# Where the gamma folds, two sums of x and the Strassen weight sums sit among the first fifteen slots of a fused cross-attention kernel

## The chip, the cores and the metric

The kernel runs on one core of one Trainium2 chip. The metric is the device time of one execution in microseconds (us). The engines are named as in the profile: PE is TensorE (PEld its weight loads), DVE is VectorE, ACT is ScalarE, POOL is GpSimd, SP is the engine that issues most of the DMAs (SPq is its queue). Each engine executes its instructions in the order in which the kernel writes them; engines wait for one another through semaphores.

## The reference

All data is fp32. `x` is 8 x 256 x 1024, `ctx` is 8 x 256 x 1024 and serves as keys and values of 32 heads of 32 columns.

```python
mu, var = mean(x), variance(x)                       # over the last axis
xn   = (x - mu) * rsqrt(var + 1e-5) * ln_gamma + ln_beta
Q    = split_heads(xn @ Wq.T)
K    = V = split_heads(ctx)
s    = einsum('bhsd,bhtd->bhst', Q, K) * 32 ** -0.5  # masked by mask_BxS2_bf1
attn = einsum('bhst,bhtd->bhsd', softmax(s), V)
out  = x + merge_heads(attn) @ Wout.T
```

## The kernel before

**Slots.** The work is cut into N = 64 slots: 8 batches of NQ = 8 groups of four heads. The loop `for n in range(N)` (L938) writes the instructions of all engines by hand, in the order in which they run (a manual schedule). Slot n does this, in this order:

- PE: `scores(n + 1)` (L485, 16 matmuls into four PSUM banks tagged "sc", one for each head), steps of the output projection of an earlier batch (`product_steps`, L704), `values(n - 2)` (L630, the products with V), then query projections for later slots (`make_q`, L336, or `query_product`, L444).
- `softmax(n + 1)` (L506). For each head j the DVE adds the mask and takes the minimum (`exps`, L530), ACT takes the exponent and its sum (L534), DVE takes the reciprocal (L541), POOL multiplies by it (L548, `normalize`; in slots up to 13 head 3 is done by ACT, L544), DVE transposes 32 x 32 blocks into `pT` (`blocks`, L554), ACT copies half of them aside (`aside`, L560), and SP moves blocks between partitions in four DMAs (L616, L620). The last part, `tail`, is written behind the first `exps` of the next softmax as long as n is under 8, and at once from n = 8 on. A list `fill` holds other work, dealt out one item at a time between these steps.
- Behind the softmax come, in this order: sums of attention outputs (`sum_at`, L698, POOL), layer norm of later x (`ln_stats`, L217, DVE with a small power on POOL, L235; `ln_norm` on ACT, L248), moves of x blocks by SP (`move_x`, L321), saves of weight sums to DRAM (`keep_wq`, L405, SP), sums of x (`sum_x`, L436, POOL), the fold (`fold`, L364, POOL) and the weight sums listed in `sums[n]` (L850 to L864).

A head's PSUM bank of scores is free for the next slot's scores once its two L530 instructions have read it; there are four banks, and each slot fills all four.

**Gamma.** Batch 0 multiplies by gamma where x is transposed (`copy_x0`). From batch 1 on the scaled gamma is folded into `wq`, in place, when batch 0 has used a block of it. `fold(o)` does row block o in one POOL instruction of 128 x 1024; it is called at the end of slots 0 to 3 for o = n. Row blocks 4 to 7 are done by `fold_late`, eight DVE instructions of 128 x 512 (L373), as items of `fill` in slots 4 and 5.

**Strassen.** The output projection and, from batch 2 on, the query projection are 2 x 2 block products with seven multiplications (Strassen-Winograd). The sums of weight blocks T1 to T4 are made once: `sum_wo` (L182, for Wout) and `sum_wq` (L403, for Wq), each an elementwise 128 x 512 instruction, on the engine that the lists name. The sums of x (S1, S2, S4, S3 of `sum_x`, L442, 128 x 512 each) are made for every batch from 2 on. Batch 2's query products run in slots 10 (S1), 11 (S4), 12, 13 (S2), 14 (S3), 15 and 16; batch 0's output projection runs in slots 9 to 16.

**Slots 8 to 10 around the change.** In slot 8 the two x sums S1 and S2 of batch 2 stand at the end, behind the DMAs of `move_x` that slot 7 issues. Slot 9 ends with two wo sums on DVE (L182) and two wq sums on POOL (L403). In slot 10 `add_p1` (L755, POOL) adds a kept product to the residual tile `r`, `store` (L764, DVE) adds the PSUM bank "po" to the same tile, and only then may the next four projection steps (`po_S`, L722) overwrite that bank.

Of the kernel before, what the change touches and what calls it, by code (L numbers as in the profile page):

```python
# [49 lines left out]
ALU = mybir.AluOpType  # L50
# [9 lines left out]
def xattn_kernel(  # L60
# [10 lines left out]
    nc = tc.nc  # L71
# [4 lines left out]
    NQ = NC  # L76
# [8 lines left out]
    NEG_SCALE = -1.0 / math.sqrt(HD)  # L85
# [21 lines left out]
    NK = D // P // 2  # L107
# [134 lines left out]
    def ln_norm(b, s, engine):  # L242
        if engine is nc.scalar:
            shift = sm.tile([P, 1], F32, tag="shift", name=f"shift_{b}_{s}", bufs=2)
            nc.gpsimd.tensor_scalar(
                shift, mvs[b][:, s, 0:1], rstds[b][:, s : s + 1], -1.0, ALU.mult, ALU.mult
            )
            engine.activation(  # L248
                xs[b][:, s, :], xs[b][:, s, :], AF.Identity,
                bias=shift, scale=rstds[b][:, s : s + 1],  # L250
            )
            return
        engine.tensor_scalar(
            xs[b][:, s, :], xs[b][:, s, :], mvs[b][:, s, 0:1], rstds[b][:, s : s + 1],
            ALU.subtract, ALU.mult,
        )
# [107 lines left out]
    def fold(o):  # L364

        nc.gpsimd.tensor_tensor(
            wq[:, o], wq[:, o], gs.unsqueeze(2).to_broadcast([P, NC, P]), ALU.mult
        )

    def fold_late(*chunks):  # L370

        for c in chunks:
            nc.vector.tensor_scalar(  # L373
                wq[:, ds(NK, NK), c], wq[:, ds(NK, NK), c], gs[:, c : c + 1], None, ALU.mult
            )

# [471 lines left out]
    sums = {n: [] for n in range(N)}  # L850
    for n, engine, which, *chunks in (
        (1, nc.gpsimd, T3, 0), (2, nc.gpsimd, T3, 1), (4, nc.gpsimd, T2, 0, 1),
        (4, nc.gpsimd, T3, 2), (5, nc.gpsimd, T3, 3), (5, nc.gpsimd, T2, 2, 3),
        (6, nc.gpsimd, T4, 0), (7, nc.gpsimd, T4, 1), (9, nc.vector, T4, 2, 3),
        (10, nc.vector, T1, 0, 1), (13, nc.gpsimd, T1, 2), (14, nc.gpsimd, T1, 3),
    ):
        sums[n] += [partial(sum_wo, which, c, engine) for c in chunks]
    for n, engine, which, *chunks in (
        (6, nc.gpsimd, "T1", 0, 1), (7, nc.gpsimd, "T1", 2, 3), (9, nc.gpsimd, "T2", 0, 1),
        (10, nc.gpsimd, "T2", 2), (11, nc.gpsimd, "T2", 3), (11, nc.gpsimd, "T3", 0),  # L860
        (12, nc.gpsimd, "T3", 1, 2), (13, nc.gpsimd, "T3", 3), (13, nc.vector, "T4", 0),
        (14, nc.vector, "T4", 1, 2), (14, nc.gpsimd, "T4", 3),
    ):
        sums[n] += [partial(sum_wq, which, o, engine) for o in chunks]  # L864

# [3 lines left out]

    away, rings = {n: [] for n in range(N)}, {n: [] for n in range(N)}  # L870
    for n, name, half in (
        (7, "T1", 0), (8, "T1", 1), (9, "B11", 0), (10, "B11", 1), (13, "T3", 0), (14, "T3", 1),
    ):
        away[n].append(partial(keep_wq, name, half))
    for n, b in firsts.items():
# [37 lines left out]
    for _ in first:  # L913
        pass
    ln_norm(1, 1, nc.vector)


    steps, evacuations = {}, {n: [] for n in range(N + 1)}
# [19 lines left out]
    for n in range(N):  # L938
        b, i = divmod(n - NQ, NQ)
        new_q = new_qs[n]  # L940
        between = []
        if n % 2 and n + 1 < N:
            between.append(partial(load_v, n + 1))
        elif n % 2 == 0 and n + 4 < N:
            between.append(partial(load_k, n + 4))
        ahead = rings[n]
        if n + 3 in firsts or n + 2 in firsts:
            between, ahead = between + ahead, []
        if b >= 0:
            if b == B - 2 and i - 1 in (5, 6):  # L950
                between.append(partial(send, b, *ENDS_TO[i - 1]))
            if i < 4:
                between.append(partial(load_res, b, *((0, 0), (0, 1), (1, 1), (1, 0))[i]))
        between += [partial(load_x, *args) for args in loads[n]]
        between += [partial(load_mask, one) for one in masks[n]]
        if n in (3, 4):
            between.append(partial(load_wo, B21, n - 3))
        if n == N - 4:
            again = xp.tile([P, NS, D], F32, tag="x", name="x_again")
            for s in range(NS):  # L960
                between.append(partial(nc.sync.dma_start, again[:, s, :], x[B - 1, ts(s, P), :]))

        if n + 1 < N:
            scores(n + 1)
        project_steps(n, 0)
        hooks, now, behind = {}, [], []
        for what, one, *args in evacuations[n]:
            if one == B - 2:
                now.append(partial(what, one, *args))
            else:  # L970
                place = 0 if i in (3, 4, 6) or i < 3 and what is not add_p1 else "soon" if i == 2 else 1
                hooks.setdefault(place, []).append(partial(what, one, *args))
        if n >= 2:
            values(n - 2)
        project_steps(n, 1)
        copies = [partial(copy_q, q) for q in new_q]
        if n in halves and n % 2 == 0:
            make_q(halves[n], second=True, chunks=range(NC // 2, NC))
            copies.insert(0, partial(copy_q, halves[n]))
        behind_p1 = new_q if i == 1 and b in P1_ASIDE else ()  # L980
        if behind_p1:
            copies = []
        else:
            for q in new_q:
                make_q(q)
        if n in products:
            query_product(*products[n])
            copies.append(partial(copy_product, *products[n]))
        for one in now:
            one()  # L990
        fill = []
        if n < 2:
            transpose_x1(2 * n)
            transpose_x1(2 * n + 1)
            fill = [partial(copy_x1, 2 * n), partial(copy_x1, 2 * n + 1)]
            if n == 1:
                hooks["soon"], fill = fill, []
        elif n <= NQ:
            fill = [partial(ln_stats, *args, parts=(i,)) for args in stats[n] for i in range(3)]
            fill += [partial(blocks_x, *args) for args in trans[n]]  # L1000
            fill += [partial(fold_late, *chunks) for chunks in {4: ((0, 1), (2, 3), (4, 5)), 5: ((6, 7),)}.get(n, ())]
        if n + 1 < N:
            softmax(n + 1, copies, ahead, between, hooks, fill)
            for q in behind_p1:
                make_q(q)
                copy_q(q)
        else:
            copy_at(n - 2)
            tails.pop()()
            for load in between:  # L1010
                load()
        if b >= 0 and i == 1:
            sum_at(b, "S2", *((slice(NK - 1, NK),) if b == B - 2 else ()))
        later = []
        if n > NQ:
            for args in stats[n]:
                ln_stats(*args, later=later)
        for args in norms[n]:
            ln_norm(*args, nc.scalar)
        if n > NQ:  # L1020
            for args in trans[n]:
                blocks_x(*args)
        for args in moves[n]:
            move_x(*args)
        for one in away[n]:
            one()
        for one in biases[n]:
            mask_bias(one)
        project_steps(n, 2)
        for one, slot in S3_SLOTS:  # L1030
            if n == slot:
                sum_at(one, "S3")
        if b >= 0:
            for name in {2: ("S4",), 3 if b == B - 2 else 5: ("S1",)}.get(i, ()):
                sum_at(b, name)
            if i == 0 and b == B - 2:
                sum_at(b, "S2", slice(0, NK - 1))
        for slot, name in ((n + 2, "S1"), (n + 2, "S2"), (n + 1, "S4"), (n - 1, "S3")):
            if slot in firsts:
                sum_x(firsts[slot], name)  # L1040
        if b == B - 2:
            if i > 2:
                add_kept(b, i, *ENDS_TO[i])
        elif b >= 0 and i in (3, 4, 5):
            add_p1(b, *{3: (0, 1), 4: (1, 1), 5: (1, 0)}[i])
        for one in later:
            one()
        if n in halves and n % 2:
            make_q(halves[n], second=True, chunks=range(NC // 2))
        if n == 0:  # L1050
            nc.gpsimd.tensor_scalar(gs, gam, NEG_SCALE, 1.0, ALU.mult, ALU.mult)
        if n < NK:
            fold(n)
        for one in sums[n]:
            one()
        if N - NQ + 2 < n < N - 1:

            c = n - (N - NQ + 3)
            if c == 0:
                last = ps_q.tile([P, 512], F32, tag="pq", name="po_last")  # L1060
            end_steps(last, "A11", B11, (c,), (0,))
# [101 lines left out]
```

## Time and profile before

| | us |
|---|---|
| median of 3 runs (580.30 to 580.79) | 580.46 |
| the profiled execution | 581.39 |
| its span, first to last instruction | 579.6 |
| mean granted TensorE clock, share of full | 0.991 |
| PE busy in the span | 569.3 (98%) |
| DVE busy | 473.1 (82%) |
| ACT busy | 423.7 (73%) |
| POOL busy | 389.5 (67%) |

The span is shorter than the profiled execution's own time by 1.8 us, which lie around it. The slots can be read off the PE timeline: each begins with 16 matmuls of L493. Slots 2 to 17 begin at 36.01, 43.59, 51.15, 58.69, 67.06, 80.02, 87.56, 95.10, 103.47, 117.01, 126.38, 134.88, 143.42, 151.93, 161.23 and 168.88 us, with slot 18 at 177.24. PE's busy time is modelled, so its share is read together with these beginnings. In the table by stretch the columns are the stretch, its length, then for PE, PEld, DVE, ACT and POOL the busy time with the instructions in brackets, then the granted clock, the DMA share and GB/s.

### The profile page before, as it was taken

To read this page: it belongs to the slowest core of one execution; us is meant where nothing else is said; L and a number is where in the kernel's file an instruction comes from. 1 tells how busy PE (TensorE), PEld (TensorE's weight loads), DVE (VectorE), ACT (ScalarE), POOL (GpSimd) and SP (SyncE) were. 2 spreads that over 40 slices of the span, in tenths; PEclk is the share of its full clock that TensorE was granted. 3 is DMA by queue.
4 is the path that set the end of the run, shared out by engine and by line. 5 is a ranking of instruction groups with operands and counts; after the bars stand their busy time and mean duration, and the time that the engine had idled before them with its cause. 6 is when DMAs were issued, how large, how long until landed. Compare 5 with 4: busy or idle time off the path is not lost.

```text
span 579.6 us, 20202 instructions
## 1 busy us (share of the span) xinstructions
PE 569.3 (98%) x7266; PEld 398.5 (69%) x7266; DVE 473.1 (82%) x1715; ACT 423.7 (73%) x1462; POOL 389.5 (67%) x643
## 2 busy tenths in 40 slices
PE   9999999799999999999999999999999999999997
PEld 8788686567766776667776777767776677665544
DVE  5988988798998888978889788988888768879823
ACT  3699699597677876778676886779677767769920
POOL 2477696978678665857749756686656666458780
PEclk9999889999999999999999999999999999999999
DMA  8964568744878658887668676887657855435751
GB/s 309 396 176 144 161 180 259 245 138 137 264 245 268 181 155 234 242 255 213 196 199 249 213 222 185 241 232 221 188 172 225 276 162 161 136 111 172 219 160 72
DMA packets 47219, 119.02 MB, mean 205 GB/s; under 512 B 8976, under 2 KB 9744, under 8 KB 47120
## 3 DMA queue, kind: packets, MB, share of 16 engines
q1 hardware_dynamic: 46976, 117.74, 67.9%
q8 instruction: 57, 0.93, 0.7%
q14 instruction: 42, 0.34, 0.2%
q10 hardware_dynamic: 144, 0.01, 0.0%
HBM read 66.33 MB, written 11.53 MB: 134 GB/s over the span
## 4 chain that ended last, share of the span: by engine, by line
PE 75%; DVE 7%; DMA 5%; POOL 5%; ACT 4%; issue 2%; SPq 2%; POOLq 0%; ACTq 0%; DVEq 0%
PE po_S L722 19%; PE pq_A L454 16%; PE sc L493 10%; PE pv L638 9%; PE po_A L722 8%; PE pq_S L454 6%; ACT e L534 3%; PE po_end L789 3%; DVE pT L554 2%; POOL e L548 2%; DVE e L530 2%; DMA xnT<-xe 2%; DMA pT<-pT 1%; DMA r<-in_x_dram 1%; PE po_last L789 1%
## 5 line engine op out<-in xcount | busy, mean ns | idle before, releaser
L548 POOL TENSOR_SCALAR e<-e,rden 128x256 f32<-128x256 f32 x484 | 225.1, 483 | 139.8 <-DVE rden L541 135.2
L534 ACT ACTIVATE e<-e,mn 128x256 f32<-128x256 f32 x512 | 254.0, 501 | 53.9 <-DVE mn L530 52.8
L554 DVE STREAM_TRANSPOSE pT<-e 128x512 f32<-128x512 f32 x256 | 179.3, 704 | 38.1 <-POOL e L548 33.6
L530 DVE CUSTOM_DVE_ANT_0 e<-sc,mb 128x256 f32<-128x256 f32 x512 | 185.4, 416 | 25.1 <-PE sc L493 25.1
L560 ACT COPY pc<-pT 128x512 f32<-128x512 f32 x128 | 78.9, 617 | 57.8 <-DVE pT L554 35.7
L534 ACT ACTIVATION_READ_ACCUMULATOR e<-e,mn 128x1 f32 x512 | 98.2, 192 | 0.0
L493 PEld LDWEIGHTS sc<-k,qa 32*128 32x128 f32 x1024 | 47.8, 185 | 44.9 <-issue 19.5
L493 PE MATMUL sc<-k,qa 32*128 32x256 f32 x1024 | 76.7, 404 | 1.2 <-DVE mn L530 1.1
L722 PE MATMUL po_S<-wo,at 128*128 128x512 f32 x152 | 74.4, 606 | 0.5 <-DVE r L764 0.5
L638 PE MATMUL pv<-pT,v 64*32 64x128 f32 x4096 | 74.9, 276 | 0.0
L638 PEld LDWEIGHTS pv<-pT,v 64*32 64x32 f32 x4096 | 57.6, 106 | 22.8 <-issue 11.8
L722 PE MATMUL po_A<-wo,at 128*128 128x512 f32 x128 | 59.4, 605 | 0.0
L345 PE MATMUL pq<-xnT,wq 128*128 128x256 f32 (+1 forms) x240 | 55.9, 388 | 0.2 <-POOL e L548 0.2
L722 PE MATMUL po_S<-wo,s 128*128 128x512 f32 x104 | 51.8, 623 | 4.1 <-DVE r L764 4.1
L454 PEld LDWEIGHTS pq_A<-xnT,wq 128*128 128x128 f32 x416 | 48.5, 192 | 6.2 <-issue 5.0
L345 PEld LDWEIGHTS pq<-xnT,wq 128*128 128x128 f32 x240 | 45.3, 193 | 8.9 <-issue 1.7
L454 PE MATMUL pq_A<-xnT,wq 128*128 128x128 f32 x416 | 48.5, 275 | 0.0
L541 DVE RECIPROCAL rden<-den 128x2 f32<-128x2 f32 x256 | 38.1, 150 | 11.7 <-ACT e L534 10.6
L530 DVE DVE_READ_ACCUMULATOR2_ANT mn<- 128x1 f32 x512 | 42.4, 83 | 0.0
L722 PEld LDWEIGHTS po_A<-wo,at 128*128 128x128 f32 x128 | 22.9, 189 | 25.7 <-issue 24.7
L722 PEld LDWEIGHTS po_S<-wo,at 128*128 128x128 f32 x152 | 25.5, 190 | 20.3 <-issue 19.5
L755 POOL TENSOR_TENSOR r<-r,p 128x512 f32<-128x512 f32 x24 | 30.6, 1276 | 5.6 <-DMA r<-in_x_dram 5.6
(104 smaller groups left out, 658.6 us busy)
## 6 DMA issues: line engine op xcount, KB each, us to landing
v<-in_kv_dram SPq DMA_DIRECT2D x32, 512.0 KB, 4.0
pT<-pT SPq DMA_DIRECT2D x128, 128.0 KB, 3.0
pT<-pc SPq DMA_DIRECT2D x128, 128.0 KB, 3.9
ring<-kept_T SPq DMA_DIRECT2D x20, 512.0 KB, 4.9
k<-in_kv_dram SPq DMA_DIRECT2D x32, 256.0 KB, 4.0
x<-in_x_dram SPq DMA_DIRECT2D x15, 512.0 KB, 5.9
r<-in_x_dram SPq DMA_DIRECT2D x28, 256.0 KB, 4.7
out_dram<-r SPq DMA_DIRECT2D x28, 256.0 KB, 3.6
```

What stands on the lines that cost most here:

```text
L345: nc.tensor.matmul(pqs[n], wq[:, o, c, :], xnTs[b](c), start=(c == 0), stop=(c == NC - 1),)
L454: nc.tensor.matmul(pqs[b][:, o, :], w[:, c], x_[:, c], start=begins and o + c == 0, stop=c == NK - 1, skip_group_check=True,)
L493: nc.tensor.matmul(scs[n][j][:, s, :], qa[r, n % NQ, ts(s, P)], ks[n - n % 2][r, n % 2, :], start=True, stop=True,)
L530: nc.vector.tensor_tensor_reduce(out=e[:, s, :], in0=pss[j][:, s, :], in1=mbs[n // NQ], scale=1.0, scalar=NO_SCORE, op0=ALU.add, op1=ALU.m ...
L534: nc.scalar.activation(e[:, s, :], e[:, s, :], AF.Exp, bias=mn[:, s : s + 1], scale=-1.0, accum_out=den[:, s : s + 1],)
L541: nc.vector.reciprocal(rden, dens[j])
L548: nc.gpsimd.tensor_scalar(es[j][:, s, :], es[j][:, s, :], rden[:, s : s + 1], 1.0, ALU.mult, ALU.mult,)
L554: nc.vector.transpose(pT[:, :, :, j, :, :].rearrange("p a i s k -> p (a i) s k"), es[j].rearrange("p s (b t) -> p b s t", t=K),)
L560: nc.scalar.copy(pc[:, :, ts(j, 2)], pT[:, 1, :, ts(j, 2)])
L638: nc.tensor.matmul(pvs[n][r][j * HD : (j + 1) * HD], vs[n - n % 2][ts(r, 2 * K), i, ds(n % 2 * P + j * HD, HD)], pT[ts(r, 2 * K), :, i, j, ...
L722: nc.tensor.matmul(po, operand(b, name)[:, c], wo[:, which, c], start=begins and c == 0, stop=c == NK - 1, skip_group_check=not begins,)
L755: nc.gpsimd.tensor_tensor(r, r, p1s[b], ALU.add)
```

## The change

`fold_late` goes. All eight row blocks are folded by POOL: blocks 0 and 1 (and the small scaled gamma that they need) right before the loop, behind the first softmax, and block n + 2 at the end of slots 0 to 5. For batch 2 alone, S1 and S2 of x move from the end of slot 8 to that of slot 9, and S4 from slot 9 to 10; S3 stays in slot 11. The weight sums are dealt anew: DVE does six of wo's sixteen in place of four (three in slot 9, two in slot 10, one in slot 12), POOL ten in place of twelve, and several wq sums on POOL change slots. The save of the first half of wq's T1 moves from slot 7 to slot 8.

```diff
-    def fold_late(*chunks):
-
-        for c in chunks:
-            nc.vector.tensor_scalar(
-                wq[:, ds(NK, NK), c], wq[:, ds(NK, NK), c], gs[:, c : c + 1], None, ALU.mult
-            )
...
     for n, engine, which, *chunks in (
         (1, nc.gpsimd, T3, 0), (2, nc.gpsimd, T3, 1), (4, nc.gpsimd, T2, 0, 1),
-        (4, nc.gpsimd, T3, 2), (5, nc.gpsimd, T3, 3), (5, nc.gpsimd, T2, 2, 3),
-        (6, nc.gpsimd, T4, 0), (7, nc.gpsimd, T4, 1), (9, nc.vector, T4, 2, 3),
-        (10, nc.vector, T1, 0, 1), (13, nc.gpsimd, T1, 2), (14, nc.gpsimd, T1, 3),
+        (5, nc.gpsimd, T3, 2, 3), (6, nc.gpsimd, T2, 2, 3), (9, nc.vector, T4, 0, 1, 2),
+        (10, nc.vector, T4, 3), (10, nc.vector, T1, 0), (12, nc.vector, T1, 1),
+        (13, nc.gpsimd, T1, 2), (14, nc.gpsimd, T1, 3),
     ):
         sums[n] += [partial(sum_wo, which, c, engine) for c in chunks]
     for n, engine, which, *chunks in (
-        (6, nc.gpsimd, "T1", 0, 1), (7, nc.gpsimd, "T1", 2, 3), (9, nc.gpsimd, "T2", 0, 1),
-        (10, nc.gpsimd, "T2", 2), (11, nc.gpsimd, "T2", 3), (11, nc.gpsimd, "T3", 0),
-        (12, nc.gpsimd, "T3", 1, 2), (13, nc.gpsimd, "T3", 3), (13, nc.vector, "T4", 0),
-        (14, nc.vector, "T4", 1, 2), (14, nc.gpsimd, "T4", 3),
+        (6, nc.gpsimd, "T1", 0), (7, nc.gpsimd, "T1", 1, 2, 3), (8, nc.gpsimd, "T2", 0, 1),
+        (11, nc.gpsimd, "T2", 2, 3), (12, nc.gpsimd, "T3", 0, 1, 2), (13, nc.gpsimd, "T3", 3),
+        (13, nc.vector, "T4", 0), (14, nc.vector, "T4", 1, 2), (14, nc.gpsimd, "T4", 3),
     ):
         sums[n] += [partial(sum_wq, which, o, engine) for o in chunks]
...
-        (7, "T1", 0), (8, "T1", 1), (9, "B11", 0), (10, "B11", 1), (13, "T3", 0), (14, "T3", 1),
+        (8, "T1", 0), (8, "T1", 1), (9, "B11", 0), (10, "B11", 1), (13, "T3", 0), (14, "T3", 1),
...
     ln_norm(1, 1, nc.vector)
+    nc.gpsimd.tensor_scalar(gs, gam, NEG_SCALE, 1.0, ALU.mult, ALU.mult)
+    for o in range(2):
+        fold(o)
...
-            fill += [partial(fold_late, *chunks) for chunks in {4: ((0, 1), (2, 3), (4, 5)), 5: ((6, 7),)}.get(n, ())]
...
-        for slot, name in ((n + 2, "S1"), (n + 2, "S2"), (n + 1, "S4"), (n - 1, "S3")):
-            if slot in firsts:
-                sum_x(firsts[slot], name)
+        for slot, one in firsts.items():
+            late = 1 if one == SPLIT else 0
+            for name in {-2: ("S1", "S2"), -1: ("S4",)}.get(n - slot - late, ()) + {1: ("S3",)}.get(n - slot, ()):
+                sum_x(one, name)
...
-        if n == 0:
-            nc.gpsimd.tensor_scalar(gs, gam, NEG_SCALE, 1.0, ALU.mult, ALU.mult)
-        if n < NK:
-            fold(n)
+        if n + 2 < NQ:
+            fold(n + 2)
```

Here `firsts` maps the slot of a batch's first query product to the batch (10 to batch 2), `SPLIT` is 2, `NK` is 4 and `NQ` is 8.

## The prediction

> **What bounds the kernel now.** I read the waits of PE first, then the busy times by slot, then the timeline of the two bad places and the chain that ended last. PE waits for little that the profile can name:
>
> ```profile
> PE po_S L722 <- DVE r L764: 4.7, 3, 3.3
> PE busy L119 <- POOL ring masks.py:199: 1.4, 1, 1.4
> PE sc L493 <- DVE mn L530: 1.1, 2, 0.6
> ```
>
> Busy times by slot (cut at the first score matmul of slots 5, 6, 7, 10 and 18) say more:
>
> ```profile
> core 0: us, PE busy (x) PEld busy (x) DVE busy (x) ACT busy (x) POOL busy (x), PEclk, DMA share, GB/s
> ...
> 58.69:67.06 8.37, 7.65 (x105) 6.09 (x104) 8.37 (x17) 3.98 (x13) 6.11 (x7) 1.00 0.57 174
> 67.06:80.02 12.96, 12.36 (x104) 9.02 (x105) 11.92 (x47) 11.61 (x43) 10.08 (x16) 0.74 0.64 177
> 80.02:87.56 7.54, 7.54 (x106) 6.09 (x105) 6.21 (x27) 7.43 (x26) 6.67 (x10) 1.00 0.58 152
> ...
> 103.47:117.01 13.54, 10.24 (x119) 6.80 (x118) 11.93 (x38) 8.77 (x30) 13.00 (x18) 0.87 0.65 217
> ...
> 177.24:185.75 8.51, 8.51 (x119) 6.24 (x118) 7.78 (x29) 5.96 (x22) 7.75 (x12) 1.00 0.83 250
> ```
>
> Slots 5, 6 and 7 hold the same matmuls (about 105), but only slot 7 runs at PE's own pace, 7.54 us, as slots 2 to 4 and 8 do. Slots 5 and 6 take 58.69 to 80.02 = 21.33 us where two such slots take 15.08: **6.25 us lost**, most of it at a granted clock of 0.74. Slot 10 has the matmuls of slot 18 (x119) but takes 13.54 against 8.51: **5.03 us lost**, of which 3.30 are idle and 1.48 are the next four po_S steps, slowed (3.46 against 1.98 in slot 11). Nearly everywhere else up to slot 18 PE follows PE; slot 15 idles for 0.53. So the profile offers at most 6.25 + 5.03 + 0.53 = 11.8 us, and other engines matter only where they hold up PE.
>
> Slot 5, in the timeline (start, length, engine, line):
>
> ```profile
> 61.55 4.09 POOL L182 TENSOR_TENSOR wo<-wo 128x512 f32<-128x512 f32 x3
> 61.85 2.66 DVE L373 TENSOR_SCALAR wq<-wq,gs 128x512 f32<-128x512 f32 x2
> ...
> 65.06 1.26 DVE L373 TENSOR_SCALAR wq<-wq,gs 128x512 f32<-128x512 f32 x2
> 66.25 0.41 DVE L530 CUSTOM_DVE_ANT_0 e<-sc,mb 128x256 f32<-128x256 f32 x1
> ...
> 67.06 0.69 PE L493 MATMUL sc<-k,qa 32*128 32x256 f32 x2 [0.55 <-DVE mn L530]
> ```
>
> The late folds keep DVE from the scores that PE finished at 59.84; PE then lacks free banks at 67.06. A fold takes 0.46 us alone, but 1.26 and 1.48 beside POOL's sums: the two engines alternate here, each waiting for the other's instruction. Slot 10, in the chain:
>
> ```profile
> 97.09 2.55 DMA xnT<-xe
> ...
> 109.06 2.56 POOL wq L403 x2
> ...
> 112.88 0.70 DVE r L764
> ```
>
> POOL waits for the x blocks until 99.76 (3.18 us idle), makes S1 and S2 (2.54 us), and only then normalizes softmax 10, whose first reciprocal had been ready at 98.49. DVE idles 3.94 us, starts softmax 11 at 109.17 and ends the store at 113.57; PE wanted the bank at 110.3.
>
> **The change, part by part.** All times continue the profiled execution; an estimated slot n starts at PE's pace.
>
> *DVE folds out.* Eight instructions go: 1.09 + 2.66 + 1.26 + 1.09 = 6.10 us. DVE's last but one transpose of softmax 5 then needs only POOL's third normalize (60.33 + 0.94 = 61.27) and ends at 62.0; softmax 6 starts there, not at 66.25. With a transpose of 0.68 and eight L530 at 0.345 it has read all banks by 65.5; PE wants them at 58.69 + 7.55 = 66.24. The stall goes with 0.7 us to spare. What stays: PE's idle 0.17 at 61.09, where a PSUM bank is freed by an ACT copy that ends at 60.95 either way. **Gain 6.25 - 0.17 = 6.1.** If the spare time is gone, each us beyond it comes back.
>
> *Folds on POOL.* Four more of 1.90 us. Slots 0 to 3 hold one each before and after. The two ahead of the loop plus 0.20 for the scaled gamma run from 23.86 to about 27.9, where softmax 1 wants POOL at 27.24: 0.6 late, hidden, since DVE may trail PE's slot start by about 4 us before scores wait and trails by 2.67 in slot 2; uncovered, 0.6. Slots 4 and 5 trade three sums (3.84) for two sums and a fold (4.46); with six normalizes (2.76) that is 7.22 of 7.55 us, and slots 6 and 7 hold 6.6 as before. Walking POOL, DVE and ACT through with their rows, I get the third normalize of softmax 6 to 10 ending near 68.5, 75.7, 82.5, 89.2 and 96.6, and DVE trailing PE's slot start by 3.3, 3.1, 3.1, 2.8 and 2.0 in slots 5 to 9. So PE keeps its pace with some 0.7 to 1.2 us to spare, but DVE reaches slot 9 about 0.8 later, against PE, than now (96.26 - 95.10 = 1.16). Slot 8's last query copy on ACT ends near 91.4 where PE wants its bank at 88.87 + 2.16 = 91.03: **cost 0.4**.
>
> The rows say a fold costs POOL 1.90 and DVE two instructions of 0.46. The Trainium skill (GPSIMD Engine Reference, section 4.1, Engine selection) says the same against this change: elementwise work with two inputs belongs on VectorE, GpSimd being about twice as slow. By it the move adds 4 x 1.90 - 8 x 0.46 = 3.9 us of engine time; as a cost in the sum that would halve the gain, but it falls on an engine with slack.
>
> *Sums of x a slot later.* In front of softmax 10's normalizes the 3.18 wait and 2.54 of S1 and S2 go; two wq sums (2.56) come in. S1 and S2 then follow the normalizes and one `sum_at`: 96.6 + 1.28 + 1.27 = 99.1 for S1. PE wants S1 after 16 scores, values and two steps, 3.1 into slot 10 (97.24 + 0.4 + 3.1 = 100.7): 1.6 to spare. The x blocks land long before (99.64, less the 6.2 that slot 7 moves up). S4 ends near 109.7; PE wants it about 112. Late, each costs its lateness.
>
> *Three wo sums on DVE in slot 9.* DVE ends softmax 10's transposes near 98.5, the statistics (1.6) at 100.1, then T4's three sums: alone 3 x 0.68. Beside them POOL runs S2, the small power and `add_p1`; a sum caught by one of POOL's took 1.76 (slot 10 now). So softmax 11 starts between 102.2 and 103.4. From its start to the store's end now takes 4.4, less 0.81 for `add_p1`, which comes earlier: 3.6 to 3.9. The bank is free at 106.1 to 107.3, where PE wants it at 104.35: **a stall of 1.8 to 3.0 stays, I take 2.4**.
>
> An idle 3.30 was followed here by a clock of 0.76 (111 to 118 us); an idle 0.53 by 1.00. 2.4 us is nearer the first, so I take its share of the slowing, 1.48 x 2.4 / 3.3 = 1.1, between 0 and 1.5. The skill (TensorE: Matmul & The Clock Gate, section What's actually happening) has the clock fall only after an idle window of about 3.4 us; by it that 1.1 would be zero and the time 1.1 lower. Without it: **gain in slot 10 5.03 - 2.4 - 1.1 = 1.5**, between 0.5 and 3.2.
>
> *One wo sum on DVE in slot 12.* 0.68 alone, 1.76 beside POOL's three T3 sums. DVE idles 0.24 and 0.38 at the next two slot starts, and batch 2's last query copy (151.50) leaves 0.43 until slot 15's scores. Bounds 0 and 0.9; **I take 0.3**, nearer the uncaught row.
>
> *The rest.* The save moved to slot 8 is one SP issue of 0.53. SP now issues softmax 9's first block move at 98.93 though ACT's copy ended at 96.56, behind six moves of x and that save; taking the save away there helps, and behind slot 8's moves it has until slot 9's copy, with values read two slots later. Cost nothing; were SP full, 0.5. T2 and T1 of wq keep their count per slot within one: nothing.
>
> **Sum.** -6.1 + 0.4 - 1.5 + 0.3 = -6.9. 581.39 - 6.9 = 574.5 for such an execution; the median shown lies 0.93 lower: **573.6**. With the terms' bounds this case spans 571.9 to 575.5.
>
> **Rivals.** *Both stalls go* (22%). If DVE and POOL reach slot 9 as punctual as now and the three sums slip between POOL's, the store is done before 104.35: -6.1 - 5.0 + 0.3 = -10.8, 569.7, down to 568.7 with the 0.53 of slot 15 and no other cost. For it: POOL waits 0.4 for work even in slot 8 now. Against: the added folds.
>
> *Slot 10 gets no better or worse* (15%). DVE's three sums alternate with POOL's each time, or S1 is late too: the stall stays at 3.3 or grows by up to 2. Gain 6.1 less 0.6 to 3: 575 to 577.5.
>
> *The stall only moves* (5%): softmax 6 to 9 trail by over 4 and scores wait in slots 6 to 9 for about what slots 5 and 6 lose now: 579.4 to 581.5.
>
> *POOL becomes the bound: slower* (6%). Its sums grew to 1.72 and its normalizes from 0.47 to 0.63 where DVE's work met them. If all of slots 4 to 9 went so, three two-input instructions and six normalizes would add 3 x 0.44 + 6 x 0.16 = 2.3 us to 7.2, and PE would follow at 9.5 a slot: 6 x 2.0 = 12 us, with slot 10's 5 kept, against 11.3 lost now: about 586. It decides against the change once POOL needs over 7.54 + 11.3 / 6 = 9.4 us a slot. Against it: with the DVE folds gone, nothing on DVE in slots 4 to 8 slowed POOL's rows (0.47, 1.28).
>
> That leaves 52% for the forecast. Faster by over 0.2% (about what a measurement of this kernel can tell from no change) 0.52 + 0.22 + 0.15 = 0.89; within it 0.05; slower 0.06. The range for eight in ten takes in both rivals beside the forecast: 568.7 to 577.5.
>
> **What would show it.** Right: slots 5 and 6 at about 7.6 us with a clock of 1.00, no PE wait for DVE mn; POOL without a wait for the x blocks; slot 10 between 9.5 and 12 us, PE's wait for L764 there near 2.4, and L182 on DVE in slot 9 with one near 1.8. Wrong: PE waiting for S1 (pq_S for POOL sx) in slot 10, for mn in slots 6 to 8, or slot 10 at 8.5.

## The result, and the profile after

The changed kernel takes 574.69 us (median of 4 runs, 574.50 to 574.84) against 580.38 for the kernel before on the same chip: the ratio is 0.9905, with a 95% interval of 0.9888 to 0.9922. In a later comparison on one chip it took 574.56 against 581.41 (ratio 0.9882, 0.9850 to 0.9915). The profiled execution took 574.59 with a span of 572.8, 6.8 less than before. Line numbers after L366 are 7 lower in the changed kernel: L523 is the old L530 (minimum), L541 the old L548 (normalize), L486 the scores, L715 the projection steps, L748 `add_p1`, L757 the store, L435 the sums of x.

PE's waits in the changed kernel, in total, times, longest:

```profile
PE po_S L715 <- DVE r L757: 3.3, 2, 2.8
PE busy L119 <- POOL ring masks.py:199: 1.3, 1, 1.3
PE pq L345 <- ACT qa L354: 0.7, 1, 0.7
PE po_A L715 <- ACT qa L354: 0.4, 1, 0.4
```

The wait for DVE's mn is gone; the one for the store (2.8 at its longest) is not, and two waits for ACT's query copies have come. The same stretches as before, cut at the first score matmul of slots 5, 6, 9, 10, 11 and 12:

```profile
core 0: us, PE busy (x) PEld busy (x) DVE busy (x) ACT busy (x) POOL busy (x), PEclk, DMA share, GB/s
58.49:66.73 8.24, 7.59 (x106) 6.09 (x105) 7.87 (x27) 8.07 (x30) 7.04 (x9) 1.00 0.76 220
66.73:74.27 7.54, 7.54 (x106) 6.09 (x105) 6.30 (x26) 7.00 (x26) 7.54 (x11) 1.00 0.74 211
...
89.36:98.21 8.85, 8.44 (x96) 4.19 (x95) 7.42 (x30) 8.62 (x30) 8.19 (x13) 1.00 0.73 205
98.21:110.39 12.18, 9.41 (x119) 6.31 (x118) 11.43 (x33) 6.34 (x23) 8.89 (x13) 0.94 0.89 312
110.39:120.71 10.32, 10.32 (x122) 7.13 (x121) 9.69 (x30) 9.72 (x32) 7.04 (x11) 0.90 0.52 155
```

Slot 6 fell from 12.96 to 7.54, PE's own pace, at full clock. Slot 10 fell only from 13.54 to 12.18, and slot 11 grew from 9.37 to 10.32, at a clock of 0.90. In slot 5, DVE now follows POOL's last normalize at once, while the fold runs on POOL:

```profile
61.51 1.90 POOL L366 TENSOR_TENSOR wq<-wq,gs 128x1024 f32<-128x1024 f32 x1
61.58 0.71 DVE L547 STREAM_TRANSPOSE pT<-e 128x512 f32<-128x512 f32 x1 [0.26 <-POOL e L541]
...
62.22 0.38 DVE L523 CUSTOM_DVE_ANT_0 e<-sc,mb 128x256 f32<-128x256 f32 x1
...
66.73 1.15 PE L486 MATMUL sc<-k,qa 32*128 32x256 f32 x16
```

Softmax 6 starts at 62.22 (66.25 before) and the 16 score matmuls run in one piece (67.06 to 71.86 before). Where slot 10 stands still is in the timeline of slots 9 and 10:

```profile
100.27 1.26 POOL L435 TENSOR_TENSOR sx<-sx,xnT 128x512 f32<-128x512 f32 x1
100.57 3.79 DVE L182 TENSOR_TENSOR wo<-wo 128x512 f32<-128x512 f32 x3
101.49 1.00 POOL L235 TENSOR_TENSOR rstd<-ve,mhalf 128x1 f32<-128x1 f32 x1
102.46 1.35 POOL L748 TENSOR_TENSOR r<-r,p 128x512 f32<-128x512 f32 x1
...
107.10 0.68 DVE L757 TENSOR_TENSOR r<-po_A,r 128x512 f32<-128x512 f32 x1
107.84 2.62 PE L715 MATMUL po_S<-wo,s 128*128 128x512 f32 x4 [2.77 <-DVE r L757]
```

DVE's three T4 sums take 3.79 us. One by one (shortest, median and longest in ns):

```profile
L182 DVE TENSOR_TENSOR wo<-wo x3: 678/1508/1755, 100.6 to 102.6; 128x512 f32<-128x512 f32 x3
```

The first (1.51) ends 0.55 behind POOL's S2, the second (0.68) runs beside POOL's small power, and the third (1.76) ends 0.55 behind `add_p1`: two of the three are caught by a two-input instruction of POOL. Softmax 11 starts at 104.28, the store ends at 107.78, and PE has waited 2.77 us for it. POOL no longer waits for the x blocks. Behind the wait the granted clock (last but two) is halved for about 3.4 us, which slot 10's end and slot 11's beginning pay:

```profile
104.00:108.00 4.00, 1.23 (x11) 1.04 (x10) 4.00 (x21) 3.20 (x14) 0.98 (x3) 1.00 0.87 284
108.00:110.00 2.00, 2.00 (x4) 0.51 (x4) 1.31 (x5) 1.77 (x8) 2.00 (x6) 0.76 0.97 367
110.00:112.00 2.00, 2.00 (x17) 1.22 (x16) 2.00 (x4) 2.00 (x7) 2.00 (x3) 0.50 0.09 35
112.00:114.00 2.00, 2.00 (x73) 1.19 (x66) 2.00 (x4) 1.64 (x3) 0.94 (x1) 0.89 0.27 59
```

### The profile page after: what moved, and what is told of

The parts are those of the page before. It is cut to its first block, busy times and chain, and to the rows that moved or that the text cites. A ratio compares the mean times of both kernels' runs of the same rounds, so it can differ in the third digit from the quotient of the medians.

```text
span 572.8 us, 20206 instructions
## 1 busy us (share of the span) xinstructions
PE 564.1 (98%) x7266; PEld 395.2 (69%) x7266; DVE 470.5 (82%) x1709; ACT 423.4 (74%) x1462; POOL 393.0 (69%) x645
## 4 chain that ended last, share of the span: by engine, by line
PE 78%; DVE 7%; POOL 6%; ACT 3%; DMA 3%; issue 2%; SPq 0%; POOLq 0%; DVEq 0%; ACTq 0%
PE po_S L715 19%; PE pq_A L447 16%; PE pv L631 10%; PE po_A L715 9%; PE sc L486 9%; PE pq_S L447 7%; POOL e L541 3%; PE po_end L782 3%; DVE e L523 2%; ACT e L527 2%; DVE pT L547 2%; POOL wq L366 2%; DMA pT<-pT 1%; PE po_last L782 1%; PE busy L119 1%
## 5 line engine op out<-in xcount | busy, mean ns | idle before, releaser
L541 POOL TENSOR_SCALAR e<-e,rden 128x256 f32<-128x256 f32 x484 | 223.3, 478 | 137.6 <-DVE rden L534 135.1
L523 DVE CUSTOM_DVE_ANT_0 e<-sc,mb 128x256 f32<-128x256 f32 x512 | 185.4, 416 | 27.5 <-PE sc L486 27.3
L486 PEld LDWEIGHTS sc<-k,qa 32*128 32x128 f32 x1024 | 46.6, 186 | 42.9 <-issue 21.2
L715 PE MATMUL po_S<-wo,at 128*128 128x512 f32 x152 | 74.4, 606 | 0.5 <-DVE r L757 0.5
L486 PE MATMUL sc<-k,qa 32*128 32x256 f32 x1024 | 74.6, 405 | 0.1
L715 PE MATMUL po_A<-wo,at 128*128 128x512 f32 x128 | 59.4, 605 | 0.4 <-ACT qa L354 0.4
L715 PE MATMUL po_S<-wo,s 128*128 128x512 f32 x104 | 50.8, 613 | 2.8 <-DVE r L757 2.8
L523 DVE DVE_READ_ACCUMULATOR2_ANT mn<- 128x1 f32 x512 | 42.4, 83 | 0.0
L715 PEld LDWEIGHTS po_A<-wo,at 128*128 128x128 f32 x128 | 22.9, 189 | 26.1 <-issue 24.5
L715 PEld LDWEIGHTS po_S<-wo,at 128*128 128x128 f32 x152 | 25.5, 190 | 20.3 <-issue 19.5
L644 ACT COPY at<-pv 128x128 f32<-128x128 f32 x128 | 26.2, 253 | 8.9 <-PE pv L631 8.9
```

The source lines that it names most:

```text
L486: nc.tensor.matmul(scs[n][j][:, s, :], qa[r, n % NQ, ts(s, P)], ks[n - n % 2][r, n % 2, :], start=True, stop=True,)
L523: nc.vector.tensor_tensor_reduce(out=e[:, s, :], in0=pss[j][:, s, :], in1=mbs[n // NQ], scale=1.0, scalar=NO_SCORE, op0=ALU.add, op1=ALU.m ...
L541: nc.gpsimd.tensor_scalar(es[j][:, s, :], es[j][:, s, :], rden[:, s : s + 1], 1.0, ALU.mult, ALU.mult,)
L644: nc.scalar.copy(ats[b, k][:, c, :, ts(r, 2), :], pv.rearrange("p a s k -> p s a k"))
L715: nc.tensor.matmul(po, operand(b, name)[:, c], wo[:, which, c], start=begins and c == 0, stop=c == NK - 1, skip_group_check=not begins,)
```

## Experiments

Two theories stood against each other. **A:** the gain is the scores' stall of slots 5 and 6, made by DVE's folds; POOL's place in the following slots, and DVE's sums in slot 9, decide how much of it is kept. **B:** the gain comes from the x sums that no longer wait in slot 8. Rivals for single points are named in the expectations. All kernels compute the whole result. The kernels ran on several chips, each beside the kernel before, so ratios compare better than medians. Slot lengths are those of one profiled execution of each kernel, read off the PE timeline from one first score matmul to the next:

| kernel | median us | ratio to before (95%) | slot 5 | 6 | 7 | 8 | 9 | 10 | 11 | 12 to 15 |
|---|---|---|---|---|---|---|---|---|---|---|
| before | 580.46 | 1 | 8.37 | 12.96 | 7.54 | 7.54 | 8.37 | 13.54 | 9.37 | 34.85 |
| before, again | 580.92 (one run) | | 8.42 | 13.45 | 7.61 | 7.53 | 8.37 | 13.83 | 9.47 | 34.82 |
| changed | 574.69 | 0.9905 (0.9888 to 0.9922) | 8.24 | 7.54 | 7.55 | 7.54 | 8.85 | 12.18 | 10.32 | 34.82 |
| changed, again | 574.56 | 0.9882 (0.9850 to 0.9915) | 8.12 | 7.54 | 7.54 | 7.54 | 8.85 | 12.94 | 9.37 | 34.82 |
| folds only | 578.86 | 0.9956 (0.9940 to 0.9973) | 8.17 | 7.54 | 7.83 | 8.63 | 9.88 | 15.05 | 9.45 | 34.81 |
| x sums only | 576.36 | 0.9923 (0.9903 to 0.9943) | 8.36 | 10.25 | 8.07 | 7.54 | 9.08 | 10.08 | 9.37 | 35.42 |
| changed, folds undone | 578.15 | 0.9953 (0.9936 to 0.9970) | 7.95 | 10.26 | 8.06 | 7.54 | 9.07 | 12.22 | 10.32 | 34.81 |
| changed, no folds ahead | 578.10 | 0.9944 (0.9929 to 0.9958) | 7.74 | 7.54 | 8.45 | 9.26 | 9.87 | 13.34 | 10.45 | 34.80 |
| T4 in slot 11 | 574.02 | 0.9892 (0.9867 to 0.9917) | 8.04 | 7.54 | 7.54 | 7.54 | 8.85 | 8.51 | 9.36 | 39.06 |
| one T4 less in slot 9 | 573.01 | 0.9859 (0.9836 to 0.9882) | 8.21 | 7.54 | 7.54 | 7.54 | 8.86 | 9.87 | 9.37 | 36.35 |
| T4 spread | 571.19 | 0.9835 (0.9806 to 0.9865) | 8.21 | 7.59 | 7.54 | 7.54 | 8.80 | 8.51 | 9.37 | 35.66 |
| T4 spread, norm later | 571.90 | 0.9839 (0.9820 to 0.9858) | 7.54 | 7.59 | 7.54 | 7.54 | 9.25 | 8.51 | 9.69 | 36.59 |
| T4 spread, wq's T4 earlier | 572.21 | 0.9844 (0.9817 to 0.9872) | 8.22 | 7.54 | 7.56 | 7.55 | 8.83 | 8.51 | 9.36 | 36.74 |

**Folds only.** The kernel before, with the folds as in the change:

```diff
+    nc.gpsimd.tensor_scalar(gs, gam, NEG_SCALE, 1.0, ALU.mult, ALU.mult)
+    for o in range(2):
+        fold(o)
...
-            fill += [partial(fold_late, *chunks) for chunks in {4: ((0, 1), (2, 3), (4, 5)), 5: ((6, 7),)}.get(n, ())]
...
-        if n == 0:
-            nc.gpsimd.tensor_scalar(gs, gam, NEG_SCALE, 1.0, ALU.mult, ALU.mult)
-        if n < NK:
-            fold(n)
+        if n + 2 < NQ:
+            fold(n + 2)
```

> The kernel before with the fold part alone: all eight folds on POOL (two ahead of the loop, then one in each of slots 0 to 5), x sums and weight sums as before. Theory A (the gain is the scores' stall of slots 5 and 6, which DVE's folds made): slots 5 and 6 near 7.6 to 8.3 us each, 4 to 6 us of the gain, 574.5 to 576.5 us, less if POOL, which now holds a fold and three sums in slots 4 and 5 (8.5 us of 7.55), trails so far that scores wait later. Slot 10 stays at 12 to 14 us. Rival B (the gain comes from the x sums that no longer wait for their DMA in slot 8): no gain, 579.5 to 581.

It gained 0.4%: 578.86 lies between the ranges of A (with its condition that POOL may trail) and B. Slots 5 and 6 took 8.17 and 7.54, so DVE's folds did make that stall; but slots 7 to 10 grew by 0.29, 1.09, 1.51 and 1.51 = 4.4 us and gave most of it back (slot 10, 15.05, was to stay at 12 to 14). POOL shows why:

```profile
61.81 1.90 POOL L366 TENSOR_TENSOR wq<-wq,gs 128x1024 f32<-128x1024 f32 x1
63.66 3.74 POOL L182 TENSOR_TENSOR wo<-wo 128x512 f32<-128x512 f32 x3
67.39 2.74 POOL L548 TENSOR_SCALAR e<-e,rden 128x256 f32<-128x256 f32 x6
70.09 1.90 POOL L366 TENSOR_TENSOR wq<-wq,gs 128x1024 f32<-128x1024 f32 x1
71.95 3.73 POOL L182 TENSOR_TENSOR wo<-wo 128x512 f32<-128x512 f32 x3
75.66 2.75 POOL L548 TENSOR_SCALAR e<-e,rden 128x256 f32<-128x256 f32 x6
```

There is no gap from 61.81 to 78.41: a period is 1.90 + 3.74 + 2.74 = 8.3 us where PE's slot is 7.54. In the changed kernel it is 7.1, from 61.51 to 68.60.

**X sums only.** The kernel before, with S1, S2 and S4 of batch 2 one slot later (the hunk of the change on `firsts`, no other):

```diff
-        for slot, name in ((n + 2, "S1"), (n + 2, "S2"), (n + 1, "S4"), (n - 1, "S3")):
-            if slot in firsts:
-                sum_x(firsts[slot], name)
+        for slot, one in firsts.items():
+            late = 1 if one == SPLIT else 0
+            for name in {-2: ("S1", "S2"), -1: ("S4",)}.get(n - slot - late, ()) + {1: ("S3",)}.get(n - slot, ()):
+                sum_x(one, name)
```

> The kernel before with the x-sum part alone: batch 2's S1, S2 and S4 one slot later, folds and weight sums as before. Theory A: slots 5 and 6 together stay at 21.3 us, POOL's 3.2 us wait for the x blocks goes, DVE with only two weight sums in slot 9 reaches the store in time, slot 10 falls from 13.5 to between 8.5 and 10: 575.4 to 577. Rival B: the same gain or more, 574 to 575.5, and it is the change's whole gain. Rival C (the x sums only move POOL's work, and add_p1 behind them holds the store as before): slot 10 stays above 12, 579.5 to 581.

It gained 0.8%. Slot 10 fell from 13.54 to 10.08: the 3.2 us wait of POOL is gone, softmax 11 starts at 105.73, but POOL's `add_p1` still stands behind two sums of x and two of wq and ends only at 109.41, so PE waits 1.3 us:

```profile
109.44 0.69 DVE L764 TENSOR_TENSOR r<-po_A,r 128x512 f32<-128x512 f32 x1 [0.82 <-POOL r L755]
...
110.19 1.98 PE L722 MATMUL po_S<-wo,s 128*128 128x512 f32 x4 [1.31 <-DVE r L764]
```

The time, 576.36, is in A's range, and C is refuted. But A has the time for a reason in part wrong: it let slots 5 and 6 stay at 21.3 us. Here slots 5 to 7 took 26.68 in place of 28.87, though nothing is changed up to slot 8, with the same two waits of 0.55 and 0.60 for mn. The difference is the granted clock, last but two in these rows, first of this kernel, then of the kernel before, again:

```profile
69.00:71.00 2.00, 1.95 (x21) 1.11 (x28) 2.00 (x10) 2.00 (x10) 1.81 (x4) 1.00 0.67 143
71.00:73.00 2.00, 2.00 (x69) 1.70 (x65) 2.00 (x7) 1.25 (x6) 1.26 (x4) 1.00 0.97 308
73.00:75.00 2.00, 2.00 (x11) 1.77 (x10) 2.00 (x7) 1.83 (x6) 2.00 (x3) 1.00 0.98 275
```

```profile
69.00:71.00 2.00, 1.94 (x12) 0.86 (x11) 2.00 (x7) 2.00 (x9) 1.72 (x4) 0.76 0.74 169
71.00:73.00 2.00, 2.00 (x66) 1.60 (x65) 2.00 (x7) 1.24 (x5) 1.53 (x3) 0.50 0.96 328
73.00:75.00 2.00, 2.00 (x5) 1.64 (x6) 2.00 (x8) 1.83 (x6) 2.00 (x2) 0.50 0.90 262
```

So some 2.2 to 2.8 us of the kernel before's loss in slots 5 to 7 goes with a halved clock behind the stall, which not every execution meets. A second profile of the kernel before shows whether its own executions differ in this.

> The kernel before once more, for a second profile. If the 6.25 us lost in slots 5 and 6 are partly the clock gate (0.50 from 69 to 75 us in the first profile, 1.00 with the same waits where only later slots differ), this profile shows slots 5 to 7 between 26.3 and 28.9 us together, with waits of DVE mn of 1.1 us either way. If the clock falls in every execution of this kernel, 28.5 to 29 again.

It gave 29.48 us for slots 5 to 7 with the clock at 0.50, near the second case. The clock fell in both profiles of the kernel before and in neither of the two others with DVE's folds (x sums only with the same two waits, folds undone with one of 0.60). The mean clocks of the other runs say more. A clock halved for 6.8 us, as in both profiles of the kernel before, takes about 0.006 off the mean (an estimate, 3.4 of 580). Of the four runs of x sums only, two have a mean of 0.994 (576.82 and 577.18 us) and two of 0.997 and 1.00 (575.46 and 575.90). Of 32 executions of the kernel before in the later comparisons, three have 0.996 or 0.997, and they are the three fastest (579.58 to 579.89); the others have 0.988 to 0.994 and take 580.57 to 584.43. So the same kernel meets the fall in some executions and not in others; why the kernel before meets it more often stays open.

**Folds undone.** The changed kernel with the fold part taken back (`fold_late` in slots 4 and 5, `fold(n)` in slots 0 to 3):

```diff
-    nc.gpsimd.tensor_scalar(gs, gam, NEG_SCALE, 1.0, ALU.mult, ALU.mult)
-    for o in range(2):
-        fold(o)
...
+            fill += [partial(fold_late, *chunks) for chunks in {4: ((0, 1), (2, 3), (4, 5)), 5: ((6, 7),)}.get(n, ())]
...
-        if n + 2 < NQ:
-            fold(n + 2)
+        if n == 0:
+            nc.gpsimd.tensor_scalar(gs, gam, NEG_SCALE, 1.0, ALU.mult, ALU.mult)
+        if n < NK:
+            fold(n)
```

> The changed kernel with the fold part alone undone: folds 0 to 3 on POOL in slots 0 to 3, blocks 4 to 7 by the eight DVE instructions in slots 4 and 5; x sums and weight sums as changed. Theory A: slots 5 and 6 together back at about 21 us; slot 10 keeps a stall of about 2 us from the three DVE sums: 578.5 to 580.5. Rival B: as the changed kernel, 574 to 575.5.

578.15: just under A's range (578.5 to 580.5) and far from B's, which is refuted. A had slots 5 and 6 back at 21 us; they took 18.21, as the clock stayed at 1.00. Slots 5 to 7 are 26.27 in place of 23.33, so the folds are worth 2.9 us here, and slot 10 shows the same 2.77 us wait (12.22) as the changed kernel, so that wait does not come from the folds on POOL. Nor is A the whole: without the folds the rest of the change still gained 3.1 us (581.29 to 578.15), and the x sums alone 4.9, of which 2.2 lie in the profile in slots 5 to 7, where they change nothing. In slot 9 PE waits for a query copy of ACT without the folds on POOL too; the changed kernel, then folds undone:

```profile
92.00 6.28 PE L715 MATMUL po_A<-wo,at 128*128 128x512 f32 x14 [0.41 <-ACT qa L354]
```

```profile
95.23 6.28 PE L722 MATMUL po_A<-wo,at 128*128 128x512 f32 x14 [0.64 <-ACT qa L354]
```

**No folds ahead.** The changed kernel with two blocks folded in each of slots 4 and 5 and none ahead of the loop:

```diff
-    for o in range(2):
-        fold(o)
...
-        if n + 2 < NQ:
-            fold(n + 2)
+        for o in {0: (0,), 1: (1,), 2: (2,), 3: (3,), 4: (4, 5), 5: (6, 7)}.get(n, ()):
+            fold(o)
```

> The changed kernel without the two folds ahead of the loop: POOL folds one block in each of slots 0 to 3 and two in each of slots 4 and 5, all else as changed. Theory A (POOL's place in slots 4 to 9 decides, the room ahead of the loop is free): POOL holds 2.76 + 2.56 + 3.8 = 9.1 us in slots 4 and 5 against 7.55, trails by about 3 more, slots 7 to 10 grow by 1 to 4 us in all: 576 to 579. Rival F (the place of the folds is of no weight once DVE has none): 574 to 575.5.

> The changed kernel once more, beside the next two on the same chip. 574 to 576, ratio 0.988 to 0.992.

578.10 against 574.56 on the same chip: A's range, and F is refuted. Against the changed kernel's second profile, slots 7 to 11 grew by 0.9, 1.7, 1.0, 0.4 and 1.1, as POOL's folds and sums of slot 4 take 3.75 + 2.50 where they take 1.90 + 2.52 in the changed kernel. Slot 5, however, was 0.4 to 0.5 shorter than in the changed kernel, which is the price of the two folds ahead: PE's wait there, for a query copy of ACT, is 0.46 to 0.65 us in every kernel that has them, except one that moves a norm of ACT to a later slot (below); in those without, PE idles there for 0.16 to 0.22.

**T4 in slot 11.**

```diff
-        (5, nc.gpsimd, T3, 2, 3), (6, nc.gpsimd, T2, 2, 3), (9, nc.vector, T4, 0, 1, 2),
+        (5, nc.gpsimd, T3, 2, 3), (6, nc.gpsimd, T2, 2, 3), (11, nc.vector, T4, 0, 1, 2),
```

> The changed kernel with DVE's three T4 sums moved from the end of slot 9 to that of slot 11. Theory A (slot 10's stall is those three sums, each waiting for one of POOL's two-input instructions, 3.79 us for three): softmax 11 starts near 100.6 instead of 104.3, the store ends before PE wants the bank, no wait for L757 in slot 10, slots 10 and 11 near 8.5 and 9.4 in place of 12.2 and 10.3; up to 1.5 us come back in slots 12 and 13: 570 to 572. Rival D (POOL's lateness in slots 8 and 9 makes the stall: the store waits for add_p1): the wait for L757 stays above 2 us, 574 to 575.

Slots 10 and 11 came out as A has them, with no wait for the store in slot 10 and a clock of 1.00:

```profile
98.07:106.58 8.51, 8.51 (x120) 6.25 (x119) 7.86 (x30) 6.37 (x23) 8.40 (x13) 1.00 0.94 317
106.58:115.94 9.36, 9.36 (x121) 6.62 (x120) 8.73 (x29) 8.74 (x28) 6.08 (x10) 1.00 0.83 256
```

That is 4.6 us won, and D is refuted for slot 10. But the time, 574.02, fell by only 0.5 to 0.7, less than the intervals can tell, since slots 12 to 15 took 39.06 in place of 34.82. The same sums meet POOL's wq sums in slot 11:

```profile
117.55 4.23 DVE L182 TENSOR_TENSOR wo<-wo 128x512 f32<-128x512 f32 x3
```

They take 4.23 us there (0.88, 1.75 and 1.76), softmax 13 starts late, and PE waits 1.60 in slot 12, 0.89 in slot 14 and 1.33 in slot 15: A's 1.5 us for what comes back was too little.

**One T4 less in slot 9.**

```diff
-        (5, nc.gpsimd, T3, 2, 3), (6, nc.gpsimd, T2, 2, 3), (9, nc.vector, T4, 0, 1, 2),
+        (5, nc.gpsimd, T3, 2, 3), (6, nc.gpsimd, T2, 2, 3), (9, nc.vector, T4, 0, 1), (11, nc.vector, T4, 2),
```

> The changed kernel with one of DVE's three T4 sums moved from slot 9 to slot 11. Theory A (each sum in slot 9 costs the store some 1.26 us): softmax 11 starts near 103.0 in place of 104.3, the wait for L757 in slot 10 falls from 2.8 to about 1.5, slots 10 and 11 together from 22.5 to 19.5 to 21, and one sum in slot 11 delays slot 12 by less than 0.5: 572 to 574. Rival D (the last sum is caught by add_p1 whatever the number): wait unchanged at 2.8, 574.5.

As A has it in direction and time: two sums take 2.12 (1.52 and 0.68), softmax 11 starts at 102.52, and slots 10 and 11 take 19.24, with the shorter wait:

```profile
106.07 1.99 PE L715 MATMUL po_S<-wo,s 128*128 128x512 f32 x4 [1.10 <-DVE r L757]
```

The row of sums and the wait both fell by 1.67: the sum taken away is the one that `add_p1` caught, so it cost more than the mean of 1.26. Slots 10 and 11 fell by 3.26; the rest goes with the clock, which was 1.00 behind the shorter wait. About 1.5 us came back in slots 14 and 15 (12 to 15: 36.35 in place of 34.82), which A did not have.

**T4 spread.** POOL idles in slot 11 until softmax 12's first reciprocal (109.12 to 111.98 with T4 in slot 11); two chunks go there, and DVE's two are dealt one to slot 10 and one to slot 11:

```diff
-        (5, nc.gpsimd, T3, 2, 3), (6, nc.gpsimd, T2, 2, 3), (9, nc.vector, T4, 0, 1, 2),
-        (10, nc.vector, T4, 3), (10, nc.vector, T1, 0), (12, nc.vector, T1, 1),
+        (5, nc.gpsimd, T3, 2, 3), (6, nc.gpsimd, T2, 2, 3), (10, nc.gpsimd, T4, 0, 1), (10, nc.vector, T4, 2),
+        (10, nc.vector, T1, 0), (11, nc.vector, T4, 3), (12, nc.vector, T1, 1),
```

> The changed kernel with T4 spread: chunks 0 and 1 by POOL at the end of slot 10, where it idles 2.9 us, chunk 2 by DVE in slot 10 and chunk 3 by DVE in slot 11; T1 as changed. Theory A: slots 10 and 11 as with all three in slot 11 (8.5 and 9.4), and slots 12 to 15 back at 8.5, 8.5, 8.5 and 9.3, since DVE is caught once in slot 11 and not three times: 569.5 to 571.5. Rival E (POOL, with two sums more in slot 10, delays softmax 12 and the stall only moves on to slots 11 to 13): 572.5 to 574.5.

571.19, within A's range, E refuted, and the fastest of all: 1.65% below the kernel before and, by the medians, about 3.4 us below the changed one. Slot 15 alone is not as A has it (10.13 in place of 9.3). POOL's two sums fill the gap exactly:

```profile
109.04 2.97 POOL L182 TENSOR_TENSOR wo<-wo 128x512 f32<-128x512 f32 x2
111.97 0.94 POOL L541 TENSOR_SCALAR e<-e,rden 128x256 f32<-128x256 f32 x2
```

What is left of PE's waits is 0.6 us in slot 5, 0.4 in slot 9 and 1.3 in slot 15. Two kernels went for these.

**Spread, norm later** moves the second layer norm of batch 2 on ACT from slot 3 to slot 4 (`norms=(3, 3)` to `norms=(3, 4)`).

> The spread kernel, with the second layer norm of batch 2's x on ACT one slot later (slot 4 in place of slot 3). Theory A (PE's idle 0.65 in slot 5 and 0.41 in slot 9 are ACT's two norms in slot 3, which make its query copies late): slot 5 at 7.6 in place of 8.2; slot 9 8.4 to 8.9; 0.5 to 1.1 us below the spread kernel. Rival: ACT only pays the norm in the next slot, slot 6 or 7 grows by as much, no difference.

Slot 5 fell to 7.54, so the two norms do make that wait (with the folds ahead, since without these it goes too). But slots 9, 11 and 14 grew by 0.45, 0.32 and 0.77, and nothing was won: the rival is right on the time.

**Spread, wq's T4 earlier** moves one of DVE's wq sums from slot 14 to 13 (`(13, nc.vector, "T4", 0, 1), (14, nc.vector, "T4", 2)`).

> The spread kernel with wq's T4 chunk 1 on DVE moved from slot 14 to slot 13. If slot 15's wait (1.3 us in the spread kernel) is made by DVE's two sums beside POOL's in slot 14, it falls to 0.5 or less: 570 to 571. Rival: the sum moved delays slot 14's store instead, 571 to 572.

Slot 15 fell from 10.13 to 9.70 (its wait from 1.32 to 0.73, not to 0.5) and slot 14 rose from 8.51 to 10.02, with a wait of 1.12 for the store: the rival again, at 572.21.

## Why the prediction was right, point by point

The forecast was 573.6 with a range of its own of 571.9 to 575.5; 574.69 was measured. (With the bounds that its terms name, 0.5 to 3.2 for slot 10 and 0 to 0.9 for slot 12, the sum spans 571.6 to 575.2; the result lies in both.) It was right in its mechanism for slots 5 and 6, the x sums and the stall that stays in slot 10. That its sum of 6.9 stands beside a span shorter by 6.8 is luck: up to slot 18 the profiled executions differ by only 5.7 (177.24 to 171.55), as the first medians do, and 0.83 more is a wait that no term names (below). The terms differ more than the sum does.

- *DVE folds out, 6.1.* Slots 5 and 6 went from 21.33 to 15.78: 5.55. The start of softmax 6 was forecast at 62.0 and was 62.22. The rest is slot 5's wait for a query copy, 0.65 in place of the 0.17 that "either way" was to stay. The copy ends 0.28 later, at 61.23. The folds ahead of the loop were called hidden, with a price of 0.6; POOL reached softmax 1 at 28.20 in place of 27.24, and without them slot 5 was 0.4 to 0.5 shorter. So the cover held for DVE and not for ACT, where two norms (2.4 us) leave no slack. It was also not foreseen that 2.2 to 2.8 of the 6.25 go with a clock that some executions do not lose.
- *Folds on POOL, slot 9 cost 0.4.* Measured 0.48 (8.85 against 8.37). The third normalizes of softmax 6 to 10 were put at 68.5, 75.7, 82.5, 89.2 and 96.6; they ended at 68.64, 75.70, 82.93, 90.07 and 97.72. The number and the place are right, an ACT query copy that ends late, but the cause is not shown to be the folds on POOL. The kernels that keep DVE's folds have the same wait, and longer, where PE was not slowed by the clock in slot 6 (x sums only and folds undone: 0.64, slot 9 at 9.08 and 9.07). That POOL's part rests on a balance was shown by folds only and by no folds ahead: with 8.3 us or more of POOL work in slots 4 and 5, some 4.0 to 4.4 us are lost in slots 7 to 10.
- *Sums of x a slot later, no wait.* Right: PE waited neither for S1 nor for S4.
- *Slot 10, gain 1.5.* This is the term that was mis-sized. Slots 10 and 11 together gained 13.54 + 9.37 - 12.18 - 10.32 = 0.41. That is outside its bounds of 0.5 to 3.2. The wait was 2.77 where 2.4 was taken (range 1.8 to 3.0), and what else slots 10 and 11 lost, behind the slow clock, is 12.18 + 10.32 - 8.51 - 9.37 - 2.77 = 1.85 where 1.1 was taken (bound 1.5). Two of the three sums were caught, 1.51 and 1.76, where one of 1.76 was expected. Softmax 11 so started at 104.28, 0.9 behind the latest time forecast; the wait lies in its range only because PE too came 0.7 later than forecast (105.07 in place of 104.35). T4 in slot 11 and one T4 less show the part of the sums: without them slot 10 is at 8.51, with two it is at 9.87.
- *The rule on the clock.* An idle of 2.77 us was followed by a clock of 0.50 from 110 to 112 us, and in the second profile from 108 to 110 us, where the four po_S steps took 3.38 in place of 1.98. The Trainium skill (TensorE: Matmul & The Clock Gate, section What's actually happening) puts the fall behind an idle window of about 3.4 us; here an idle shorter than that was enough, and the measurement decides. Idles of 1.10, 1.31 and 1.60 were followed by a clock of 1.00. The prediction's own measure, the length of the idle, had a row against it: slot 6 of the kernel before ran at 0.74 behind waits of 0.55 and 0.60. And the price of the slow clock is read from the profiled executions alone: two of the changed kernel's eight runs have a mean clock of 1.00 (the others 0.996 or 0.997) and are no faster, 574.84 and 575.12 against 574.25 to 574.79. What else they lost is not known.
- *Slot 12's sum on DVE, 0.3.* It took 0.65, uncaught, and slots 12 to 15 did not change (34.85 and 34.82).
- *Not in the sum.* 0.83 us of the span's difference is one wait for the store at 252.85 in the first profile of the kernel before; the second has none there.

Of the signs named, slot 6 at 7.54 with a clock of 1.00, no wait for mn, POOL without a wait for the x blocks and a T4 sum of 1.76 came true; slot 5 (8.24, not about 7.6) and slot 10 (12.18 and 12.94, not 9.5 to 12) did not. Of the rivals, both stalls going was refuted by the wait of 2.77; that slot 10 gets no better was nearly the case for that slot (0.41), with the rest of the gain kept. POOL as the bound did not come true; two experiments that load slots 4 and 5 more lost some 4 us by it, and both stayed faster than the kernel before.

## What to carry to other kernels

Work moved off an engine in one slot must be paid in the slots where the receiving engine has room: the same folds gained 2.4 us with the old sums beside them on POOL (581.29 to 578.86) and about 3.5 with the new ones (578.15 to 574.6, on different chips). These two gains lie within each other's noise, so the slots decide: with 8.3 us of POOL work in a slot of 7.54, slots 7 to 10 gave 4.4 us back. Look for the instruction in front of the one that PE waits for: three sums of 0.68 in front of a softmax took 3.8, as two of them met a two-input instruction of POOL, and dealing them one at a time, or into POOL's idle 2.9 us, was worth about half of what the whole change brought. When a profile shows a stall, compare two executions before pricing the slow clock behind it.

## What the runs showed of the hardware

- A 128x512 DVE sum of two SBUF tiles took 0.65 to 0.69 us where POOL had no two-input 128x512 instruction under way, and up to 1.77 where it met one; in slot 10 of the changed kernel both sums that did so (1.51 and 1.76) ended 0.55 behind POOL's instruction, so they seem to wait for all of it. POOL pays too: two sums of about 1.28 took 3.40 beside three of DVE's (4.23) in T4 in slot 11.
- Behind PE idles of 2.77 us and more in slot 10 (2.77 in changed, changed again, folds undone and no folds ahead; 3.30 and 3.52 in the two profiles of the kernel before; 4.72 in folds only) the clock was 0.50 for a while in all seven profiles, for 3.4 us in six and for 6.8 in no folds ahead. In no folds ahead and changed again it fell about 2.0 to 2.2 us after PE had stopped, before the idle ended (an estimate from the clock by microsecond). Behind single idles of 1.10, 1.31 and 1.60 us it stayed at 1.00.
- The clock also fell to 0.50 for 6.8 us behind two waits of 0.55 to 0.60 us between which PE had little to do, in two of the three profiled executions with both waits.
